# A two-block vision network on one core: half of the first token half's fc1 by fifteen products on quarters

## The chip, the cores and the metric

The kernel runs on one core of one Trainium2 chip. The metric is device microseconds of the whole program. The core has a matrix engine (TensorE, PE in the profile, with its weight loads as PEld), VectorE (DVE), ScalarE (ACT), GpSimd (POOL) and SyncE (SP); SP and POOL also issue transfers.

## The reference

Eight images of 384 channels and 32 x 32 points go through two layers, all in f32. Tokens are the points of an image, 1024 of them.

```
xn  = layernorm(x)                                  # over 384 channels
q, k, v = xn @ w_qkv.T + b_qkv                      # 8 heads of 48
x1  = x + softmax(q k.T / sqrt(48)) v @ w_proj.T + b_proj
h   = gelu(layernorm(x1) @ w_fc1.T + b_fc1)         # 1536 wide
x   = x1 + h @ w_fc2.T + b_fc2

y   = depthwise 7x7 convolution of x + dw_b
y   = gelu(layernorm(y) @ w1 + b1)                  # 1536 wide
y   = gamma * y * (|y| / mean |y|) + beta + y       # |y| over the tokens of a channel
out = x + y @ w2 + b2
```

## The kernel before, in words

Channels lie on the 128 partitions, three tiles of them (`CT`), and tokens along the rows. The 1536 hidden channels are twelve tiles. [...]

**Order of the work.** Python writes the instructions out in the order in which each engine runs them; there is no other scheduler. `Flow` keeps a planned time: every matrix product advances it (`flow.pe(U)`, U = 0.857 us for 512 columns), and side work is written as generators ("chains") that yield the time until their next step. A step is put into the engines' queues where the planned time has come. `flow.finish(chain)` issues all that is left of a chain at once.

**An image's round.** For image b: q and k, attention (64 steps), fc1, fc2; then w1 of image b - 1, the values of b + 1, w2 of b - 1, and so on. The convolution of an image (`convolution`, on VectorE, one tap after another over three channel tiles) is started by `start_conv` after its layer 1 is done and runs beside the next image's round, at a planned pace; `help_convolution` takes the last `HELPED` taps of each channel tile: ScalarE multiplies (`tap`), a POOL transfer adds into `acc`.

**fc1, in `mlp` (line 919).** For each token half the twelve tiles are computed by `gelu_half` (line 891): three products of 512 columns into an o bank (four of them), then ScalarE's gelu to `hid`. After tile 3 of the first half `rest()` ends attention and adds its projection (`proj`), and the layernorm of the second half is spawned (`layernorm`, line 501: sums L482 on TensorE, L525, squares, variance L482, ScalarE's L552 and L553, and three scalings L556 on VectorE). `behind_ln` is `conv_norm` (line 1770): when this layernorm has ended, `norm_of_next` starts the layernorm of the next image (four additions L1838, L1840, folds on POOL), and `end_soon` (line 1803) finishes the convolution before the layernorm of its result.

**Products by thirds.** q, k and w1 are already computed by `tiles_by_thirds` (line 422): three tiles times two token halves, in fifteen products for eighteen. The right-hand sides are sums of token halves (`make_thirds`, ten VectorE operations), the weights are sums of weight blocks (`sums_singly`, in image 0, kept in HBM as `s_qk`, `s_w1`). The products come in this order, and accumulate in four banks:

```
SINGLY = (6, 10, 3, 5, 12, 2, 0, 11, 1, 4, 14, 7, 9, 8, 13)
BANKS = {"n": (6, 5, 0, 4, 9), "z": (12, 11, 14, 8), "k": (10, 7), "q": (2, 1), "j": (3,), "m": (13,)}
```

`SUMS` says what is read from a bank after each product. Copies (`c11=n`) go to ScalarE, sums (`c31=n+c31`) to VectorE (L447, L450); j, q and m share the bank x. A product that writes to a bank waits for the last read of it.

**The shift of w1, in image 0.** `shift_through_w1` (line 1575) folds a bias through w1 in two rounds: load 1152 KB on POOL's queue, pause 22.0, six VectorE operations (L1584, L1586), two folds by POOL transfers (L1588), pause 8.0, then `two_sums` on TensorE (L287). In attention of image 0, just before the first `proj`, `attention` finishes both the `folding` and the `aside` chains, of which this is one.

**Weights.** SP loads weight chunks into a ring of nine buffers, in the order of a plan; a chunk's buffer is given back when its last product is written out (`weights.used`).

Of the kernel before, what the change touches and what calls it, by code (L numbers as in the profile page):

```python
# [67 lines left out]
HELPED = 7  # L68
# [107 lines left out]
def block_kernel(  # L176
# [11 lines left out]
    w1t: bass.AP,  # L188
    w2: bass.AP,
# [15 lines left out]
    quiet = []  # L205
    exact = [False]
# [3 lines left out]
    s_w1 = dram.tile([P, HT // CT, len(FORMS), P], F32, tag="s_w1", bufs=1, name="s_w1")  # L210

# [126 lines left out]
    def plan_fc1(tag):  # L338
        return [((f"fc1_{tag}", c), chunk(wfc1, c)) for c in range(NC)]
# [57 lines left out]
    def thirds_of(src, spare):  # L397

        b11, b12, b21, b22, b31, b32 = (src[:, s, half(n)] for s in range(CT) for n in range(2))
        f, h, e2, g = averages()  # L400
        e, f2, h2, g2, f3, d = (spare[:, s, half(n)] for s in range(CT) for n in range(2))
        steps = (
            (e, b11, b12, ALU.subtract),
            (h, e, b31, ALU.subtract),
            (e2, h, b12, ALU.add),
            (h2, h, b32, ALU.add),
            (f, e, b21, ALU.subtract),
            (g, b22, f, ALU.add),
            (g2, g, b32, ALU.add),
            (f2, f, b12, ALU.add),  # L410
            (f3, f2, g2, ALU.subtract),
            (d, g2, b31, ALU.subtract),
        )
        return steps, (b12, b21, e, b22, f, h, e2, g, b31, f2, h2, g2, f3, b32, d)

    def make_thirds(what, src, us, spare):
        steps, thirds[what] = thirds_of(src, spare)
        for step in steps:
            nc.vector.tensor_tensor(*step)
            yield us  # L420

    def tiles_by_thirds(weights, wname, g, rhs, c, banks, behind):
# [4 lines left out]
        for slot, n in enumerate(SINGLY):  # L427
# [25 lines left out]
            flow.pe(U)  # L453
# [142 lines left out]
    def large_tile(b):  # L596
        if b not in large:
            large[b] = one.tile([P, HT * N], F32, tag="big", name=f"qk_{b}")
        return large[b]

# [161 lines left out]
    def attention(b, xt, qT, kT, last_tile, ready, first, next_image):  # L762
# [44 lines left out]
        for n in range(len(steps) + 2):  # L807
            if n == 2:
                last_tile()
            if n < len(steps):  # L810
                if steps[n][0] == 0 and steps[n][2] == 0:
                    ready(steps[n][1])
                ps[n] = scores(*steps[n])
            if n >= 2:
                product(*steps[n - 2], ps.pop(n - 2))
            if n - 2 in (len(steps) // 2 - 9, len(steps) - 9):
                quiet.append("averages")
            if n - 2 == len(steps) // 2 + 6:
                for chain in first:
                    flow.finish(chain)  # L820
                xn = one.tile([P, CT, N], F32, tag="xn", bufs=2, name=f"xn2_{b}")
                for m in (NP - 1, *range(CT)):
                    flow.finish(chains[0, m])
                proj(b, xt, 0)
                quiet.clear()
                next_image(b)
                slow = {1: 1.35, B - 1: 1.2}.get(b, 1.0)
                fold = "columns" if b else None
                ln = layernorm(xt, xn, 0, eps0, "g2", f"ln2_{b}", False, spaced=True, slow=slow, fold=fold, wait=4.5)
                ln = flow.spawn(ln)  # L830
# [64 lines left out]

    def difference(dst, more, less, direct):
# [22 lines left out]
    def mlp(b, xt, xn, weights, tag, ln, rest, before_fc2=None, behind_ln=None):  # L919

        hid = one.tile([P, HT * N], F32, tag="big", name=f"hid_{b}").rearrange("p (m n) -> p m n", m=HT)
# [3 lines left out]
        for m in range(HT):  # L925
            gelu_half(hid, m, 0, xn, weights, wa, f"fc1_{b}")
            if m == 3 and rest:
                rest()
                slow = 1.2 if b == 1 else 1.0
                ln = flow.spawn(layernorm(xt, xn, 1, eps0, "g2", f"ln2_{b}", True, slow=slow))  # L930
                behind_ln(ln)
        flow.finish(ln)
# [176 lines left out]
    def convolution(acc, us, first=(), y0=0, y1=H, ready=tuple(range(CT)), taken=None, helped=0):  # L1109
# [5 lines left out]
        taps = KS * KS - helped  # L1115

        shares = [size(*divmod(i, KS), y0, y1) for i in TAPS[:taps]]
        shares = [taps * s / sum(shares) for s in shares]
        while min(done) < taps:
            left = [c for c in ready if done[c] < taps and not (taken and taken.get(c, 0) > flow.now)]  # L1120
            if not left:
# [18 lines left out]
    def help_convolution(acc, us, taken):  # L1140

        yield 8.0
        for ct in reversed(range(CT)):
            taken[ct] = float("inf")
            for i in TAPS[KS * KS - HELPED :]:
# [356 lines left out]
    def prepare(weights, aside):  # L1502
# [72 lines left out]
        def shift_through_w1():  # L1575
            for i in range(0, HT // 2, CT):
# [12 lines left out]
                yield 8.0  # L1589
# [124 lines left out]
    def main():  # L1714
# [21 lines left out]
        for b in range(1, B):  # L1736
            if b < B - 1:
                plan += plan_fc1(b) + plan_fc2_fast(b)
# [25 lines left out]
        def start_conv(b, us, *first):  # L1764
# [3 lines left out]
            state["help"] = flow.spawn(help_convolution(acc, 2.7, taken), paced=True)  # L1768
# [21 lines left out]
        def sums_for_tiles(i):  # L1790
            width = len(FORMS) * P
            spare = large[0][:, (2 * NP + 2 * i) * N : (2 * NP + 2 * i + 2) * N]
            for w, store, g in ((wqkt, s_qk, i), (w1t, s_w1, i), (w1t, s_w1, i + 2)):
                yield from sums_singly(w[:, g * width : (g + 1) * width], store[:, g : g + 1], spare)
                yield 8.0

# [121 lines left out]
        for b in range(B):  # L1918
# [9 lines left out]
            if b == 0:  # L1928
                for chain in singly:
                    flow.finish(chain)  # L1930
            if b < B - 1:
# [8 lines left out]
            if b == 0:  # L1940
                xt = load_x(b + 1, "x")
                flow.finish(preparing)
                start_conv(b, 1.6, (9, 1.65), (10, 24.0))
# [5 lines left out]
            if b < B - 1:  # L1949
                flow.finish(state["w1"])  # L1950
                y, gx = grn_up(b - 1, weights, b - 1)
                start_conv(b, 1.6 if b == B - 2 else 1.65, (23, 2.4), (24, 9.0), (25, 26.0))
# [117 lines left out]
def _arrays(i):  # L2070
# [19 lines left out]
    def in_thirds(a, places):  # L2090
# [19 lines left out]
        "w1t": in_thirds(i["L1_conv_w1"], [[4 * r + g for g in range(4)] for r in range(CT)]),  # L2110
        "w2": columns(i["L1_conv_w2"]),
# [19 lines left out]
```

## Time and profile before

| what | value |
|---|---|
| time, median of 3 runs | 3225.36 us (3224.21 to 3226.81) |
| the profiled execution's own time | 3222.53 us |
| its span, first to last instruction | 3220.8 us |
| mean granted TensorE clock | 0.999 |
| TensorE busy | 3205.4 us, 100% |
| VectorE busy | 2470.9 us, 77% |
| ScalarE busy | 1670.8 us, 52% |
| GpSimd busy | 513.1 us, 16% |
| fc1 records on TensorE (L393, `fc<-xn,fc`) | 1152 of 512 columns, 504.3 us |
| VectorE's convolution taps (L1135, `acc`) | 861, mean 1157 ns |

Lines of the profile name the engine, the source line (L393 is line 393 of the kernel), the operation and what is written from what. An f32 matrix product is two records. Records overlap in time, so a product's cost is read from the distance between starts: 0.858 us for 512 columns in a long row of them. VectorE's operations overlap a little too: a 512-column addition is shown with 0.69 us, and the next one starts 0.6 us after it.

### The profile page before, as it was taken

To read this page: it belongs to the slowest core of one execution; us is meant where nothing else is said; L and a number is where in the kernel's file an instruction comes from. 1 tells how busy PE (TensorE), PEld (TensorE's weight loads), DVE (VectorE), ACT (ScalarE), POOL (GpSimd) and SP (SyncE) were. 2 spreads that over 40 slices of the span, in tenths; PEclk is the share of its full clock that TensorE was granted. 3 is DMA by queue.
4 is the path that set the end of the run, shared out by engine and by line. 5 is a ranking of instruction groups with operands and counts; after the bars stand their busy time and mean duration, and the time that the engine had idled before them with its cause. 6 is when DMAs were issued, how large, how long until landed. Compare 5 with 4: busy or idle time off the path is not lost. (4 is left out here: it accounts for less than half of the span.)

```text
span 3220.8 us, 38808 instructions
## 1 busy us (share of the span) xinstructions
PE 3205.4 (100%) x14084; PEld 1375.1 (43%) x14084; DVE 2470.9 (77%) x3375; ACT 1670.8 (52%) x2353; POOL 513.1 (16%) x609
## 2 busy tenths in 40 slices
PE   9999999999999999999999999999999999999999
PEld 5334434443344433444344443444434444344454
DVE  4537788787877878778787687876878778879964
ACT  3542763457644475444753637637365374732543
POOL 2101211112120121201212011220121202200000
PEclk9999999999999999999999999999999999999999
DMA  6524742647335573446636375363843638433234
GB/s 217 168 82 153 167 88 58 161 111 176 80 70 157 125 157 77 95 138 153 138 66 120 113 186 107 66 130 105 200 95 59 149 98 205 73 84 90 59 119 109
DMA packets 205857, 386.64 MB, mean 120 GB/s; under 512 B 42592, under 2 KB 49120, under 8 KB 205280
## 3 DMA queue, kind: packets, MB, share of 16 engines
q0 software_dynamic: 83424, 166.76, 27.7%
q1 hardware_dynamic: 121952, 216.66, 21.9%
q8 instruction: 113, 1.85, 0.2%
q10 hardware_dynamic: 288, 0.71, 0.1%
q14 instruction: 80, 0.66, 0.1%
HBM read 201.18 MB, written 38.14 MB: 74 GB/s over the span
## 5 line engine op out<-in xcount | busy, mean ns | idle before, releaser
L1135 DVE SCALAR_TENSOR_TENSOR acc<-pad,vec,acc 128x870 f32<-128x870 f32 (+8 forms) x861 | 964.1, 1157 | 6.8 <-DMA acc<-tap 1.7
L782 ACT ACTIVATE p<-s 128x1024 f32<-128x1024 f32 x512 | 524.0, 1024 | 254.7 <-PE s L773 247.9
L773 PE MATMUL s<-qk 48*64 48x512 f32 x4096 | 537.2, 591 | 0.2 <-ACT qk L619 0.2
L793 PE MATMUL o<-p,v 64*64 64x512 f32 x4096 | 534.9, 590 | 0.0
L393 PE MATMUL fc<-xn,fc 128*128 128x512 f32 x1152 | 504.3, 594 | 0.0
L1157 POOL DMA_DIRECT2D acc<-tap x294 | 252.5, 873 | 1413.4 <-ACT tap L1156 722.8
L393 PEld LDWEIGHTS fc<-xn,fc 128*128 128x128 f32 x1152 | 217.2, 190 | 278.2 <-issue 267.7
L460 PE MATMUL fc_p<-hid,fc 128*128 128x512 f32 x728 | 316.8, 593 | 0.0
L472 ACT ACTIVATE hid<-fc,bfc_f 128x512 f32<-128x512 f32 x192 | 130.8, 684 | 331.5 <-PE fc L393 331.4
L460 PE MATMUL o_p<-y,w 128*128 128x512 f32 x664 | 289.0, 593 | 0.0
L793 PEld LDWEIGHTS o<-p,v 64*64 64x64 f32 x4096 | 162.1, 133 | 277.6 <-issue 271.7
L773 PEld LDWEIGHTS s<-qk 48*64 48x64 f32 x4096 | 158.8, 133 | 279.0 <-issue 225.4
L1156 ACT ACTIVATE tap<-pad,vec 128x512 f32<-128x512 f32 x294 | 215.8, 734 | 1.5 <-DMA acc<-tap 1.3
L460 PEld LDWEIGHTS fc_p<-hid,fc 128*128 128x128 f32 x728 | 137.8, 190 | 173.3 <-issue 168.3
L460 PEld LDWEIGHTS o_p<-y,w 128*128 128x128 f32 x664 | 125.7, 190 | 157.7 <-issue 143.4
L1135 DVE SCALAR_TENSOR_TENSOR acc_last<-pad,vec,acc_last 128x377 f32<-128x377 f32 (+24 forms) x288 | 177.3, 692 | 0.6
L734 DVE TENSOR_TENSOR attn<-o,attn 128x512 f32<-128x512 f32 x64 | 44.2, 690 | 141.2 <-ACT attn L732 141.2
L906 ACT COPY pad<-x 128x512 f32<-128x512 f32 x42 | 26.4, 634 | 196.2 <-DVE x L983 196.2
L715 PE MATMUL proj<-attn,wproj_sb 128*128 128x512 f32 x288 | 127.1, 595 | 0.0
L693 PE MATMUL v<-wv_sb,xn 128*128 128x384 f32 x384 | 126.8, 487 | 0.0
L447 DVE TENSOR_TENSOR y<-h_n,y 128x512 f32<-128x512 f32 x72 | 49.8, 692 | 64.3 <-PE h_n L431 62.0
L693 PEld LDWEIGHTS v<-wv_sb,xn 128*128 128x128 f32 x384 | 72.5, 190 | 50.1 <-issue 3.3
(397 smaller groups left out, 4089.3 us busy)
## 6 DMA issues: line engine op xcount, KB each, us to landing
acc<-tap POOLq DMA_DIRECT2D x294, 256.0 KB, 3.6
fc<-s_fc SPq DMA_DIRECT2D x91, 256.0 KB, 3.1
w<-s_w SPq DMA_DIRECT2D x91, 256.0 KB, 2.7
w<-s_w SPq DMA_DIRECT2D x72, 320.0 KB, 3.0
fc<-in_wfc SPq DMA_DIRECT2D x54, 384.0 KB, 4.4
y<-y POOLq DMA_DIRECT2D x38, 512.0 KB, 6.6
hid<-hid POOLq DMA_DIRECT2D x36, 512.0 KB, 7.2
qk<-s_qk SPq DMA_DIRECT2D x42, 320.0 KB, 4.9
```

The costliest lines, as they stand in the source:

```text
L393: nc.tensor.matmul(out=ps, lhsT=lhsT(k), rhs=rhs(k)[:, half(h)], start=(k == 0), stop=(k == nk - 1))
L447: nc.vector.tensor_tensor(c[dst], banks(name), c[other], ALU.add)
L460: nc.tensor.matmul(out=bank, lhsT=lhsT, rhs=rhs, start=k == 0, stop=k == len(pairs) - 1)
L472: nc.scalar.activation(dst, src, function, **kw)
L693: nc.tensor.matmul(out=ps[:, :C], lhsT=xn[:, k, t * P : (t + 1) * P], rhs=wv_sb[:, k, :], start=(k == 0), stop=(k == CT - 1),)
L715: nc.tensor.matmul(out=ps, lhsT=wproj_sb[:, m, ct * P : (ct + 1) * P], rhs=attn[:, m, :], start=(m == 0), stop=(m == CT - 1),)
L773: nc.tensor.matmul(out=s[64 * i : 64 * i + 64, j, :], lhsT=kT[64 * j : 64 * j + HD, m, k0 : k0 + 64], rhs=qT[64 * j : 64 * j + HD, m, half ...
L782: nc.scalar.activation(p, s, AF.Exp)
L793: nc.tensor.matmul(out=outs[i][64 * j : 64 * j + 64, :], lhsT=v[keys, t, at : at + 64], rhs=p[keys, j, :], start=(t == 0), stop=(t == KT - 1),
L1135: nc.vector.scalar_tensor_tensor(dst, window, tap, dst, ALU.mult, ALU.add)
L1156: nc.scalar.mul(t.rearrange("p (h w) -> p h w", w=W), window, tap)
L1157: nc.gpsimd.dma_start(out=acc[:, ct, half(h)], in_=t, accum_op=ALU.add)
```

## The change

Images 1 to 6 get a different fc1 for tiles 6 to 11 of the first token half. The half is cut in two quarters of 256 columns. `make_quarters` makes ten sums of quarters on VectorE, right behind the layernorm of the first half (still beside attention), into parts of the hidden tile that aren't used yet. `gelu_group` runs `tiles_by_thirds` on three tiles: fifteen products of 256 columns, with banks of two kinds (n and k in o banks, x and z in the s banks of attention); the sums land in `hid`, and gelu is taken in place. Group 0 (tiles 6 to 8) stands first, right after attention; then come plain tiles 0 to 5, with `rest()` now after tile 1; then group 1 (tiles 9 to 11). The second half stays as it was. While `hold` isn't empty (from `rest()` to tile 4) the convolution's chain issues no taps.

The weight sums for this (`sums_for_fc1`) are made in image 0, 22.0 after attention, in the tile `v`, and kept in HBM as `s_fc1`; after that POOL sets `v` to 1.0 again. Six chunks of them join the plan of each image. `hid` is now the same tile as q and k of the image.

Besides: the first of the two rounds of `shift_through_w1` pauses 18.0 rather than 8.0 between fold and sums. `HELPED` becomes 6, 7, 7 (channel tile 0 gives one tap back to VectorE). The helped taps come every 2.5 rather than 2.7, and the convolution's paces are set anew.

```diff
-HELPED = 7
+HELPED = 6, 7, 7
...
+    def fast_fc1(b):
+        return not exact[0] and 0 < b < B - 1
...
+        sums = plan_singly(f"fc1t_{tag}", s_fc1)
+        return sums[:3] + raw[:3] + sums[3:] + raw[3:]
...
+    def make_quarters(src, hid, us):
+
+        blocks = [src[:, s, quarter(n)] for s in range(CT) for n in range(2)]
+        places = [hid[:, 8 + i // 2, quarter(2 + i % 2)] for i in range(8)]
+        places[2:2] = [hid[:, 10, quarter(0)]]
+        places[6:6] = [hid[:, 10, quarter(1)]]
+        steps, thirds["fc1"] = thirds_of(blocks, places)
+        for step in steps:
+            nc.vector.tensor_tensor(*step)
+            yield us
...
                 ln = layernorm(xt, xn, 0, eps0, "g2", f"ln2_{b}", False, spaced=True, slow=slow, fold=fold, wait=4.5)
+                if fast_fc1(b):
+                    ln = sequence(ln, make_quarters(xn, hidden(b), 1.5))
...
+    def gelu_group(hid, g, b, weights):
...
+        def bank(name):
+            name = "x" if name in "jqm" else name
+            if name not in tiles:
+                make = o_tile if name in "nk" else s_tile
+                tiles[name] = make(f"fc1_{b}_{g}_{name}")[:, : NH // 2]
+            return tiles[name]
+
+        def gelu(r):
+            m = 6 + 3 * g + r
+            other_table(hid[:, m, half(0)], hid[:, m, half(0)], AF.Gelu, bias=bfc1[:, m : m + 1])
+
+        def behind(n):
+            if n == 14:
+                gelu(2)
+
+        c = {f"c{r + 1}{n + 1}": hid[:, 6 + 3 * g + r, quarter(n)] for r in range(CT) for n in range(2)}
+        for _ in tiles_by_thirds(weights, f"fc1t_{b}", g, thirds["fc1"], c, bank, behind, U / 2):
+            pass
+        gelu(1)
+        gelu(0)
...
-        for m in range(HT):
+        for m in range(HT // 2 if fast else HT):
+            if fast and m == 0:
+                gelu_group(hid, 0, b, weights)
             gelu_half(hid, m, 0, xn, weights, wa, f"fc1_{b}")
-            if m == 3 and rest:
+            if m == (1 if fast else 3) and rest:
                 rest()
                 slow = 1.2 if b == 1 else 1.0
+                if fast:
+                    hold.append(b)
                 ln = flow.spawn(layernorm(xt, xn, 1, eps0, "g2", f"ln2_{b}", True, slow=slow))
                 behind_ln(ln)
+            if m == 4:
+                hold.clear()
+        if fast:
+            gelu_group(hid, 1, b, weights)
         flow.finish(ln)
...
-            if not left:
+            if not left or hold:
                 yield 1.0
                 continue
...
-                yield 8.0
+                yield 8.0 if i else 18.0
...
-            state["help"] = flow.spawn(help_convolution(acc, 2.7, taken), paced=True)
+            state["help"] = flow.spawn(help_convolution(acc, 2.5, taken), paced=True)
...
+        def sums_for_fc1():
+            width = len(FORMS) * P
+            spare = v.rearrange("p t w -> p (t w)")
+            for g in range(2):
+                yield from sums_singly(wfc1t[:, g * width : (g + 1) * width], s_fc1[:, g : g + 1], spare)
+                yield 8.0
+            for t in range(KT):
+                nc.gpsimd.memset(v[:, t, :], 1.0)
...
+                fc1_sums = flow.spawn(after(None, sums_for_fc1(), 22.0))
...
-                start_conv(b, 1.6, (9, 1.65), (10, 24.0))
+                flow.finish(fc1_sums)
+                start_conv(b, 1.6, (9, 1.6), (10, 20.0), (48, 1.45))
...
-                start_conv(b, 1.6 if b == B - 2 else 1.65, (23, 2.4), (24, 9.0), (25, 26.0))
+                start_conv(b, 1.65 if b == B - 2 else 1.8, (23, 2.4), (24, 9.0), (25, 20.0), (62, 1.5))
```

In the changed kernel the line numbers are others: the group's products are L456, its sums L472 and L475, plain fc1 tiles L404, gelu L497, taps L1202, the layernorm's scalings L581, the next image's additions L1914 and L1916, the shift's sums L294.

## Prediction

> **What bounds the kernel now.** I read the page's busy shares first, then TensorE's own waits, then time lines of the stretches that the change touches.
>
> ```profile
> PE 3205.4 (100%) x14084; PEld 1375.1 (43%) x14084; DVE 2470.9 (77%) x3375; ACT 1670.8 (52%) x2353; POOL 513.1 (16%) x609
> ```
>
> A busy TensorE may still run below its pace, so its waits decide:
>
> ```profile
> PE b L287 <- DMA w_lnb<-w_lnb: 5.4, 1, 5.4
> PE warm L1728 <- POOL eps L1716: 1.1, 1, 1.1
> ```
>
> All its other waits are 1.0 us or less. It is the bound from end to end: a product taken out is worth its own time, and a wait put in costs its full length.
>
> In images 1 to 6 the place of the change looks like this (image 2; TensorE, then ScalarE, then VectorE; start, length, line, operation):
>
> ```profile
> 899.98 7.03 PE L393 MATMUL fc<-xn,fc 128*128 128x512 f32 x16
> 906.85 1.02 PE L482 MATMUL ln_var<-ln_sq,ones 128*128 128x512 f32 x2
> 907.70 28.49 PE L393 MATMUL fc<-xn,fc 128*128 128x512 f32 x66
> ```
>
> ```profile
> 907.75 1.28 ACT L468 ACT_TABLE_LOAD   x1
> 909.05 0.69 ACT L552 ACTIVATE ln_rstd<-ln_var,eps 128x512 f32<-128x512 f32 x1
> 909.76 0.63 ACT L553 ACTIVATE ln_rstd<-ln_rstd 128x512 f32<-128x512 f32 x1
> ```
>
> ```profile
> 910.43 2.08 DVE L556 SCALAR_TENSOR_TENSOR xn<-xn,vec,ln_rstd 128x512 f32<-128x512 f32 x3 [5.04 <-ACT ln_rstd L553]
> 912.42 1.28 DVE L1838 TENSOR_TENSOR ln<-xn 128x512 f32<-128x512 f32 x2
> 913.63 1.28 DVE L1840 TENSOR_TENSOR ln<-ln,xn 128x512 f32<-128x512 f32 x2
> 914.83 15.27 DVE L1135 SCALAR_TENSOR_TENSOR acc<-pad,vec,acc 128x899 f32<-128x899 f32 x13
> ```
>
> When the layernorm of the second token half ends, VectorE gets a block of 19.7 us in one piece (910.43 to 930.13): the scaling, four additions of the next image's layernorm, and the convolution's remaining 13 taps, which `end_soon` issues at once. TensorE meanwhile runs 66 fc1 records without a break, because plain fc1 tiles need ScalarE's gelu and nothing of VectorE. That is the cover which the change takes away.
>
> [...] after TensorE's one long wait:
>
> ```profile
> 101.54 1.04 PE L773 MATMUL s<-qk 48*64 48x512 f32 x8
> 107.97 1.96 PE L287 MATMUL b<-ones,w_lnb 64*128 64x1 f32 x12 [5.38 <-DMA w_lnb<-w_lnb]
> 109.86 1.99 PE L793 MATMUL o<-p,v 64*64 64x512 f32 x8
> 111.62 1.93 PE L773 MATMUL s<-qk 48*64 48x512 f32 x8
> ```
>
> A group of eight that takes 0.86 us elsewhere takes 1.75 here. [...] the 256-column L525 shows 418.
>
> **The parts.** TensorE's pace: w1's products by the same scheme start every 0.858 us at 512 columns. At 256 columns:
>
> ```profile
> 9.38 2.75 PE L1651 MATMUL ln_sum<-xn,ones 128*128 128x256 f32 x12
> ```
>
> Twelve records are six products; less the last one's tail of 0.17 us that is 0.430 us each. Weight loads take 190 ns, a half product 215, so they stay hidden.
>
> *Products.* Per image 18 x 0.858 = 15.44 us go, 30 x 0.430 = 12.90 come: 2.54 saved, **15.2 us** over six images (11.6 if a product takes 0.45).
>
> *Group 0*, first after attention. In the changed program's VectorE queue its eleven sums stand among the attention's last addition, a wait on `r`, a reciprocal and three taps: addition, tap, x, n, z, r-product, tap, n, reciprocal, n, tap, z and the rest (x, n, z: the bank read). Bank n is accumulated into by products 1, 4, 7, 10, 13, and each must wait until the last sum was read from it. In the trace the addition starts 0.7 us after the last attention product; start to start a 512-column operation takes 0.6, a tap 1.05, a 256-column one 0.34 (0.42 less the same overlap). x is read by 2.7 where product 6 would start at 2.15 (0.6 lost), the second n by 5.5 where product 10 would start at 4.5 (1.0), z by 7.9 where product 14 would start at 7.2 (0.7). So about 2.4 us an image, **+14.4** (6 to 21): the saving is gone here already.
>
> *Group 1, images 2 to 6.* The same queue reads, from the group's first sum: x, tap, n, z, n, tap, **three scalings, four additions, ten taps**, n, z, k, n, n, z, x. The n after the ten taps reads product 10, and product 13 waits for it. Count from the variance product (L482), 0.858 us long. Two copies out of PSUM now stand ahead of ScalarE's table load; the second waits for product 2 (read by 2.25), so the load comes at 2.25 rather than 0.90 and the scale is ready at 4.9 rather than 3.58. VectorE's own queue reaches the scalings at 6.2. Then 4.4 us (910.43 to 914.83), ten taps at 15.3/13 = 1.18 make 11.8, the n sum 0.4: 22.8. Product 13 was due at 0.858 + 12 x 0.430 = 6.0. **16.8 us an image, +84** (71 with taps at 1.05 and the scalings at 4.9; 87 at most). Queued behind product 13 are two products and the whole second half of fc1.
>
> *Group 1, image 1.* Its layernorm is slower (1.2), so the scalings stand after the last n that TensorE waits for. But the last x stands behind 17 taps, `gelu(0)` needs it, and the second half's gelus are queued behind it on ScalarE. VectorE gets to that x about 33 us after product 1. TensorE waits 1.3 us for the scalings, then fills the four o banks by 19.4, and the fifth tile waits for a gelu that comes at 34.7: **+16.6** (12 to 19).
>
> *Clock.* [...] The trace's own: work worth 0.83 + 2.14 us took 6.09 after it, 3.1 lost. **+18.6** (10 to 20).
>
> *The first fold's longer pause.* Now: TensorE waits at 102 for the fold that lands at 107.83 and 108.39; with the half clock it costs 8.7 us (114.06 against 102.43 + 2.97). Ten microseconds later the fold has long landed, so these 8.7 go. But the second round starts ten later too: its pause of 22 then ends 0.6 us after `attention` finishes the chain, so scalings, fold and sums are issued back to back just ahead of proj. In the trace they had room:
>
> ```profile
> 133.90 0.48 DVE L1584 TENSOR_SCALAR w_lnb<-w_lnb,vec 128x384 f32<-128x384 f32 x1
> ...
> 136.12 1.27 DVE L1586 SCALAR_TENSOR_TENSOR w_lnb<-w_lnb,vec 128x384 f32<-128x384 f32 x2
> 137.30 0.20 DVE L741 RECIPROCAL inv<-sums 128x8 f32<-128x8 f32 x1
> 143.93 0.69 DVE L760 TENSOR_TENSOR attn<-attn,r 128x512 f32<-128x512 f32 x1 [6.43 <-DMA r<-back]
> ```
>
> ```profile
> 137.69 1.00 POOL L1588 DMA_DIRECT2D w_lnb<-w_lnb  x1 [0.65 <-DVE inv L741]
> ```
>
> In the changed queue these scalings stand behind the last r-product, which needs reciprocal plus 6.4 us: about 134 with everything 8.7 earlier. Scalings 3.5, POOL's issue 0.3, landing some 3 us: 141. TensorE arrives at 143.86 - 8.7 = 135.2: some 6 us, and 2 to 3 of half clock. **0 net** (-6 to +6): the wait changes place.
>
> *The rest, at 0.* Quarters: ten additions of 0.34 us an image during attention, spaced by 1.5; VectorE idles 1.86 us at its end. Sums for fc1 in image 0: 40 small operations of 0.2 us, two loads and two stores of 960 KB on POOL's queue, eight memsets of 0.44; they start 22 us after attention, under fc1 tiles that don't need VectorE, and fc1 lasts 62 us; the s_w2 stores queued behind are read an image later. Without that cover up to 5. Six more weight loads an image on SP: the ring is nine deep and filled during attention. Tap counts 6, 7, 7 put one tap (1.1) more on VectorE and take two ScalarE taps (0.73) and two POOL DMAs off. Paces and hold move taps among stretches: all together -3 to +5.
>
> **Sum.** -15.2 + 14.4 + 84 + 16.6 + 18.6 + 0 = +118.4 on the profiled execution's 3222.5 (span 3220.8) gives 3340.9; the median of the runs shown is 2.8 higher, at 3225.4. I take 3342. All low ends: +78 or so, 3300; all high ends: 3370.
>
> **Rivals.** (a) *Faster*: the block on VectorE is through before the sums need it, because the convolution has no taps left when the layernorm ends. Then only the 15.2 count, or nothing after group 0: 3207 to 3222. It decides where both groups together wait 2.5 us an image; group 0 alone comes to 2.4, so past it even one tap ahead of the sums is too many, and the queue holds ten. Against it is also that the scalings ahead of them can't start before the variance product. 3%. (b) *Half a stall*: something lets n be read early, 8 us an image: 3222.5 + 118.4 - 5 x 8.8, 3297. Nothing in the queue speaks for it. 6%. (c) *More waits behind the wait*: after it fc2's products meet POOL's folds or ScalarE's backlog, 6 us an image: 3378. Against it: those steps are placed by planned time and gain slack while TensorE stands. 8%. (d) The shift's pause only moves its wait: counted above.
>
> **Numbers.** Forecast 83%; range 3300 to 3370 leaves out (a), (b), (c) and little else. About 0.2% (6.5 us) is what a measurement can tell: faster 3%, within 2%, slower 95%.
>
> **What would show it.** TensorE's waits: product L456 on VectorE's L472, five times some 16 us; in image 1 L404 on ScalarE L497, some 15. Half clock after each. VectorE: ten L1202 in one piece with an idle TensorE. Group 0: waits of 1 us or less. L294 on `w_lnb` now in the second round. A TensorE without waits over 5 us in the fc1 stretches would make this wrong.

## The result and the profile after

The changed kernel takes **3365.95 us** (median of 4 runs, 3365.05 to 3367.83), the kernel before beside it 3224.78 (3223.45 to 3226.81). The ratio is **1.0438, 95% interval 1.042 to 1.0456**: slower by 141 us. The profiled execution took 3365.05 us, its span is 3363.3.

The busy shares and the granted clock (tenths, in 40 slices) of the changed kernel's page:

```profile
PE 3226.7 (96%) x14228; PEld 1399.5 (42%) x14228; DVE 2543.0 (76%) x3610; ACT 1691.1 (50%) x2399; POOL 506.8 (15%) x607
...
PEclk9899999999989999899998999999999999999999
```

TensorE is busy for 21 us more, although 15 us of products went (worked out below), in part because some of it runs at half clock: behind the wait of image 2 shown below the granted clock was 0.50 from 965 to 969 us, 0.72 up to 971, then 1.00. A slice is 84 us; the four eights are the slices of image 0's attention and of fc1 in images 2, 3 and 4. Its waits (line, what ended the wait; us in total, times, longest):

```profile
PE fc_n L456 <- DVE qk L472: 81.2, 17, 14.5
PE fc L404 <- ACT qk L497: 14.6, 1, 14.6
PE s L801 <- ACT qk L647: 10.3, 7, 2.7
PE b L294 <- DVE attn L762: 6.6, 1, 6.6
PE b L294 <- DMA w_lnb<-w_lnb: 4.2, 2, 3.5
PE fc_z L456 <- DVE qk L472: 3.6, 5, 0.7
PE fc_x L456 <- DVE qk L472: 2.5, 6, 1.0
```

The first line holds the forecast wait for product 13, five times 14.5 us, and short waits of both groups; the second is the forecast wait for gelu in image 1. The third (L801, attention's first products, on ScalarE's L647, which adds the bias to q or k) and the fourth (L294, the sums of the shift, on VectorE's L762, an addition of attention) were not forecast. Group 1 of image 2, TensorE and then VectorE (start, length, line, operation; in brackets the idle time before it and what ended it):

```profile
949.93 0.59 PE L456 MATMUL fc_k<-qk,fc1t 128*128 128x256 f32 x2
965.03 1.22 PE L456 MATMUL fc_n<-qk,fc1t 128*128 128x256 f32 x2 [14.50 <-DVE qk L472]
966.04 1.06 PE L456 MATMUL fc_z<-xn,fc1t 128*128 128x256 f32 x2
```

```profile
949.68 2.07 DVE L581 SCALAR_TENSOR_TENSOR xn<-xn,vec,ln_rstd 128x512 f32<-128x512 f32 x3
951.67 1.29 DVE L1914 TENSOR_TENSOR ln<-xn 128x512 f32<-128x512 f32 x2
952.87 1.29 DVE L1916 TENSOR_TENSOR ln<-ln,xn 128x512 f32<-128x512 f32 x2
954.08 10.57 DVE L1202 SCALAR_TENSOR_TENSOR acc<-pad,vec,acc 128x899 f32<-128x899 f32 x10
964.55 0.42 DVE L472 TENSOR_TENSOR qk<-fc_n,qk 128x256 f32<-128x256 f32 x1
```

Product 13 starts 0.06 us after that last line ends. It waited for one sum of 0.42 us, which stood behind three scalings, four additions and ten taps, though the product that this sum reads had started at 949.07.

In image 1 the group's last sum stands behind seventeen taps, and the gelu of its tile behind that sum, and with it all later gelus, which give the o banks back (VectorE, ScalarE, TensorE):

```profile
543.99 17.86 DVE L1202 SCALAR_TENSOR_TENSOR acc<-pad,vec,acc 128x870 f32<-128x870 f32 x17
561.78 0.41 DVE L472 TENSOR_TENSOR qk<-fc_x,qk 128x256 f32<-128x256 f32 x1
```

```profile
562.23 0.72 ACT L497 ACTIVATE qk<-qk,bfc_f 128x512 f32<-128x512 f32 x1 [20.13 <-DVE qk L472]
```

```profile
563.58 2.08 PE L404 MATMUL fc<-xn,fc 128*128 128x512 f32 x2 [14.64 <-ACT qk L497]
```

To see where the 142 us lie, I compared the start of each stage on TensorE in the two traces. The lag of the changed kernel grows by:

| stage | lag gained, us |
|---|---|
| image 0, attention to fc1 | 9.45 |
| fc1 of images 1 to 6 | 17.75, 18.19, 18.79, 18.35, 18.40, 16.82: 108.3 |
| fc2 of images 1 to 6 | 2.22, then 0.5 to 0.9 each: 5.5 |
| q and k of images 2 to 7 | 1.3 to 2.7 each: 10.5 |
| attention of images 1 to 6 | 0.7 to 3.3 each: 9.3 |
| all else | -0.3 |

Of the 2.22 in fc2 of image 1 some 1.1 are work that moved there: eight records of the convolution's layernorm (L521) that stood in fc1 in the kernel before.

### The profile page after: what moved, and what is told of

Same layout as the page of the kernel before. It is cut to its first block, busy times and chain, and to the rows that moved or that the text cites. A ratio compares the mean times of both kernels' runs of the same rounds, so it can differ in the third digit from the quotient of the medians.

```text
span 3363.3 us, 39551 instructions
## 1 busy us (share of the span) xinstructions
PE 3226.7 (96%) x14228; PEld 1399.5 (42%) x14228; DVE 2543.0 (76%) x3610; ACT 1691.1 (50%) x2399; POOL 506.8 (15%) x607
## 4 chain that ended last, share of the span: by engine, by line
PE 77%; DVE 8%; issue 5%; DMA 4%; ACT 2%; POOL 1%; SPq 0%; DVEq 0%; POOLq 0%; ACTq 0%
PE fc L404 13%; PE s L801 11%; PE o L821 11%; PE fc_p L485 10%; PE o_p L485 5%; DVE acc L1202 4%; PE proj L743 4%; DMA acc<-tap 3%; PE v L721 3%; PE h_n L456 3%; PE h_z L456 2%; PE h_x L456 2%; PE o L1310 2%; PE h L391 2%; PE h_last L1359 2%
## 5 line engine op out<-in xcount | busy, mean ns | idle before, releaser
L1202 DVE SCALAR_TENSOR_TENSOR acc<-pad,vec,acc 128x930 f32<-128x930 f32 (+8 forms) x868 | 968.9, 1155 | 6.2 <-DMA acc<-tap 4.6
L801 PE MATMUL s<-qk 48*64 48x512 f32 x4096 | 547.7, 593 | 11.0 <-ACT qk L647 10.3
L404 PE MATMUL fc<-xn,fc 128*128 128x512 f32 x936 | 417.3, 601 | 14.6 <-ACT qk L497 14.6
L1224 POOL DMA_DIRECT2D acc<-tap x280 | 241.4, 875 | 1165.8 <-DVE gscale L1388 501.7
L801 PEld LDWEIGHTS s<-qk 48*64 48x64 f32 x4096 | 158.8, 133 | 297.2 <-issue 215.0
L404 PEld LDWEIGHTS fc<-xn,fc 128*128 128x128 f32 x936 | 179.7, 193 | 238.7 <-issue 218.0
L485 PE MATMUL fc_p<-qk,fc 128*128 128x512 f32 x624 | 273.6, 594 | 0.7 <-DVE qk L1050 0.7
L485 PEld LDWEIGHTS fc_p<-qk,fc 128*128 128x128 f32 x624 | 117.5, 190 | 151.4 <-issue 146.5
L1202 DVE SCALAR_TENSOR_TENSOR acc_last<-pad,vec,acc_last 128x377 f32<-128x377 f32 (+24 forms) x288 | 177.1, 688 | 0.6
L497 ACT ACTIVATE qk<-fc,bfc_f 128x512 f32<-128x512 f32 x108 | 73.8, 687 | 191.6 <-PE fc L404 191.6
L762 DVE TENSOR_TENSOR attn<-o,attn 128x512 f32<-128x512 f32 x64 | 44.1, 689 | 113.3 <-ACT attn L760 112.1
L1928 DVE SCALAR_TENSOR_TENSOR xn<-ln_sum,xn 128x256 f32<-128x256 f32 (+1 forms) x54 | 23.2, 503 | 114.6 <-PE ln_sum L1908 114.6
L456 PE MATMUL fc_n<-qk,fc1t 128*128 128x256 f32 x96 | 33.2, 430 | 77.7 <-DVE qk L472 77.7
```

What stands on the lines that cost most here:

```text
L404: nc.tensor.matmul(out=ps, lhsT=lhsT(k), rhs=rhs(k)[:, half(h)], start=(k == 0), stop=(k == nk - 1))
L456: nc.tensor.matmul(out=at, lhsT=weights.at(wname, g, slot // 5)[:, slot % 5, :], rhs=rhs[n], start=first, stop=True, skip_group_check=not ...
L485: nc.tensor.matmul(out=bank, lhsT=lhsT, rhs=rhs, start=k == 0, stop=k == len(pairs) - 1)
L497: nc.scalar.activation(dst, src, function, **kw)
L801: nc.tensor.matmul(out=s[64 * i : 64 * i + 64, j, :], lhsT=kT[64 * j : 64 * j + HD, m, k0 : k0 + 64], rhs=qT[64 * j : 64 * j + HD, m, half ...
L1202: nc.vector.scalar_tensor_tensor(dst, window, tap, dst, ALU.mult, ALU.add)
```

## The experiments

Every time below stands against runs of the kernel before on the same chip; the ratio and its 95% interval are given. Two experiments whose times are compared can stem from different chips, on which the kernel before took 3224.7 to 3226.1. "Lag" is again that of a stage against the kernel before.

### The block behind group 1

```diff
                 if fast:
                     hold.append(b)
+                    gate.append(b)
...
         if fast:
             gelu_group(hid, 1, b, weights)
+        gate.clear()
...
+        def gated(chain):
+            while gate:
+                yield 1.0
+            yield from chain
...
-                    state["norm1"] = flow.spawn(after(ln, norm_of_next(b, 22.0 if b > 1 else 28.0)))
-                    state["norm3"] = flow.spawn(after(ln, sequence(end_soon(b), norm)))
+                    state["norm1"] = flow.spawn(after(ln, gated(norm_of_next(b, 22.0 if b > 1 else 28.0))))
+                    state["norm3"] = flow.spawn(after(ln, gated(sequence(end_soon(b), norm))))
```

> The changed kernel, but the four additions of the next image's layernorm and the rest of the convolution's taps are issued only after group 1's last gelu, no longer between its sums. Theory (the wait is for the place of these steps in VectorE's queue): of the five waits of 14.9 us in images 2 to 6 only what the three scalings cost stays, some 1 to 3 us each, and image 1's 15.2 us wait for gelu goes; the half clock after them (about 3 us each) goes with them: 75 to 105 us less than the changed kernel's 3366, so 3261 to 3291. Rival (the sums of a group are too slow for fifteen products on quarters, whatever stands between them): group 1 would still wait 8 us or more an image, and the time stay above 3320. Second rival (the steps that are moved back now hold up the two layernorms after fc2): the waits of fc1 go, but TensorE waits as long further on, and the time stays above 3340.

Measured: 3283.5 us, ratio 1.0175 (1.016 to 1.0191), 82 us less than the changed kernel. TensorE's waits in this kernel (its lines stand one lower):

```profile
PE fc_n L457 <- DVE qk L473: 16.8, 17, 1.6
PE s L802 <- ACT qk L648: 8.0, 6, 2.9
PE h_n L457 <- ACT y L478: 7.0, 6, 1.2
PE b L295 <- DVE attn L763: 5.6, 1, 5.6
PE fc_p L486 <- DVE qk L1053: 4.2, 6, 0.8
```

The longest wait of fc1 falls from 14.5 to 1.6, and image 1's wait for gelu is gone. The lag of the six fc1 stages falls from 108.3 to 17.3. So the forecast mechanism holds, and the rival that the group is too slow by itself falls. The second rival is true in small: what was moved back costs 10.1 in fc2 (`fc_p`) and 7.3 in w1 (`h_n`), where the changed kernel lost 5.5 and nearly nothing. The other lags, image 0's 8.1 and 19 in q and k and attention, did not go with the fc1 waits. They have causes of their own.

### Group 0 alone

```diff
-        for m in range(HT // 2 if fast else HT):
+        for m in (*range(6), *range(9, HT)) if fast else range(HT):
...
-        if fast:
-            gelu_group(hid, 1, b, weights)
```

> The changed kernel, but tiles 9 to 11 are three plain tiles again in their old place (18 products of 512 columns); group 0, quarters, hold, paces and the longer pause stay. Theory (group 1 holds the waits): group 1's saving of 1.3 us an image goes, and its waits of 14.9 us and the half clock after them too: fc1 of images 1 to 6 is 0 to 2 us an image longer than in the kernel before. Left are image 0's 9.5 and, if they don't follow from group 1, the 20 us of q and k and attention: 3234 to 3262. Rival (group 0's own waits are larger than the 2.4 us an image of the prediction, or the layernorm that now starts after tile 1 stalls plain tiles too): above 3275.

Measured: 3265.11 us, ratio 1.0119 (1.0103 to 1.0134), 3 us above what the theory gave. The fc1 stages lag by 7.3 in all, 1.2 an image: half the products' saving, less than what group 0's waits cost. The block of ten taps is still there, as long as ever (10.56 us), but plain tiles run beside it and TensorE doesn't stop. Image 0 lags by 7.3 and q and k and attention by 24.6, the part that I had put too low.

### The convolution's numbers of before

```diff
-HELPED = 6, 7, 7
+HELPED = 7, 7, 7
...
-            state["help"] = flow.spawn(help_convolution(acc, 2.5, taken), paced=True)
+            state["help"] = flow.spawn(help_convolution(acc, 2.7, taken), paced=True)
...
-                start_conv(b, 1.6, (9, 1.6), (10, 20.0), (48, 1.45))
+                start_conv(b, 1.6, (9, 1.65), (10, 24.0))
...
-                start_conv(b, 1.65 if b == B - 2 else 1.8, (23, 2.4), (24, 9.0), (25, 20.0), (62, 1.5))
+                start_conv(b, 1.6 if b == B - 2 else 1.65, (23, 2.4), (24, 9.0), (25, 26.0))
```

> The changed kernel with the convolution's numbers of the kernel before: helped taps 7, 7, 7 every 2.7, and the old paces. The traces show the stage of q and k later by 1.3 to 2.7 us in each of images 2 to 7 and attention by 0.7 to 3.3, about 20 us in all, which the prediction had at 0. Theory A (the new paces put convolution taps where q and k's and attention's products wait for VectorE): these go, 10 to 20 us less than the changed kernel, 3346 to 3356, with no wait of L801 on L647; the block of taps in group 1 gets no shorter by more than three taps. Theory B (these small waits follow from the late layernorm and the late end of the convolution in fc1): they stay, and the time is within 6 us of 3366.

Measured: 3377.17 us, ratio 1.0469 (1.0455 to 1.0483): 11 us more than the changed kernel, where both theories had less or the same. The trace shows two things at once. No stage of q and k or of attention gains more than 0.02 us of lag: theory A is right on the waits. But fc1's lag is 138.9, 30.6 more, because of this line of VectorE in image 2:

```profile
958.72 15.26 DVE L1202 SCALAR_TENSOR_TENSOR acc<-pad,vec,acc 128x899 f32<-128x899 f32 x13
```

Thirteen taps are left for the block, not ten, and last 15.26 us, not 10.57: 4.7 more in each of five images. In image 1 it is 22 taps in 26.05 us rather than 17 in 17.86, 8.2 more. That makes 31.7, against the 30.6 seen. Here a microsecond more of block is a microsecond more of time. I had allowed for three taps, not for their longer duration (see "The help's pace").

### The pause

```diff
-                yield 8.0 if i else 18.0
+                yield 8.0
```

> The changed kernel with one edit undone: the first round of the shift through w1 pauses 8.0 again between fold and sums. The prediction put this edit at 0 (the wait changes place). The two traces show image 0 later by 9.45 us between attention's start and fc1's end. Theory (the pause causes this): 9 to 10 us less than the changed kernel, 3356 to 3357, and the wait of the sums for the first fold back at some 5.4 us. Rival (something else in image 0, such as the fc1 weight sums, causes it): within 3 us of the changed kernel's 3366.

Measured: 3362.64 us (3358.12 to 3367.51), ratio 1.0422 (1.0408 to 1.0436). The interval overlaps that of the changed kernel, so the time alone settles nothing, and the expected 9 to 10 us did not come. The profiled execution (3365.13 us, as long as the changed kernel's) shows where it went: image 0's lag falls from 9.45 to 0.65, but image 1's fc1 lags by 2.0 more, and the small waits of q and k and attention by 5.4 more (25.3 for 19.9). Why these grew isn't settled. The pause was therefore tried on the kernel before, which has none of them:

```diff
-                yield 8.0
+                yield 8.0 if i else 18.0
```

> The kernel before with one edit of the change: the first round of the shift through w1 pauses 18.0 rather than 8.0. Prediction's term: 0 (-6 to +6). Theory now (while TensorE waits for the fold, VectorE works off some twenty small operations that stood behind a reciprocal; with the longer pause TensorE arrives first, and the sums' bank is read only after them; the second round's fold is then late too): +8 to +11 us, 3233 to 3237, with a wait of L287 on VectorE's attn of 5 to 7 us near 113 and one on w_lnb of 3 to 4 near 149. Rival (it needs the fc1 weight sums or the other edits to do harm): within 3 us of the kernel before.

Measured: 3233.26 us, ratio 1.0027 (1.0016 to 1.0038), **+8.6 us for this one number** (11.6 in image 0 of the profiled execution, 3236.03 us), as the theory had it, though the first wait is longer than its 5 to 7. TensorE's waits:

```profile
PE b L287 <- DVE attn L734: 8.1, 1, 8.1
PE b L287 <- DMA w_lnb<-w_lnb: 4.0, 1, 4.0
```

The changed kernel's own trace shows the mechanism, TensorE first, then VectorE (some of the operations between are left out):

```profile
112.90 0.38 PE L294 MATMUL b<-ones,w_lnb 64*128 64x1 f32 x2
119.85 1.44 PE L294 MATMUL b<-ones,w_lnb 64*128 64x1 f32 x10 [6.57 <-DVE attn L762]
```

```profile
110.57 0.20 DVE L769 RECIPROCAL inv<-sums 128x8 f32<-128x8 f32 x1 [13.44 <-DMA sums<-attn]
...
111.25 1.87 DVE L1527 TENSOR_TENSOR qk<-qk 128x128 f32<-128x128 f32 x7
113.03 0.95 DVE L1674 TENSOR_TENSOR w_gbeta<-w_gbeta,vec 128x768 f32<-128x768 f32 x1
...
119.11 0.68 DVE L762 TENSOR_TENSOR attn<-o,attn 128x512 f32<-128x512 f32 x1
```

VectorE stands 13.44 us at a reciprocal, for a transfer. When that ends at 110.57, 29 small operations are queued up, 8.4 us of work, and behind them the addition L762, which gives back an o bank. The second of the sums' products waits for it. In the kernel before the same addition comes at the same time:

```profile
118.92 0.69 DVE L734 TENSOR_TENSOR attn<-o,attn 128x512 f32<-128x512 f32 x1 [2.06 <-ACT attn L732]
```

But there the sums stand some 10 us of attention earlier in TensorE's order, at 107.97 behind the wait for the fold, and wait for nothing of VectorE. The theory's reason is wrong in one point: the backlog isn't worked off during that wait, it runs from 107.44 to 116.9, for the most part after it. It costs nothing because TensorE, some 8.7 us late through the wait and the half clock behind it (granted clock 0.50 from 108 to 112 us, 0.53 up to 114.06), comes to the addition's own products so late that VectorE then stands 2.06 us for them. With the long pause TensorE isn't late, makes the sums behind those products, at 112.90, and stands for the addition. One delay had covered another.

### The help's pace

```diff
-            state["help"] = flow.spawn(help_convolution(acc, 2.5, taken), paced=True)
+            state["help"] = flow.spawn(help_convolution(acc, 2.7, taken), paced=True)
```

> The changed kernel with one number undone: the helped taps come every 2.7 again rather than 2.5. HELPED, the new paces, hold, both groups and the pause stay. Theory (in the traces a tap on ScalarE stands 1 to 2 us for its buffer, which a POOL addition must give back, and the copy L647 that attention's first products need is queued behind it): the waits of L801 on L647 go, the stages of q and k and of attention are each within 0.5 us of the kernel before, and the time falls by 15 to 20 us, to 3346 to 3351, with no change in the five waits for product 13. Rival (the convolution's new paces or the eighteenth tap on VectorE move these waits): the time stays within 5 us of 3366.

Measured: 3353.32 us, ratio 1.0395 (1.0381 to 1.0409). The waits of L801 on L647 are gone, and no stage of q and k or attention gains over 0.05 us: this one number caused all 19.9 us. ScalarE in the changed kernel, ahead of attention of image 2:

```profile
782.27 0.75 ACT L1223 ACTIVATE tap<-pad,vec 128x512 f32<-128x512 f32 x1 [1.05 <-DMA acc<-tap]
...
786.15 0.74 ACT L1223 ACTIVATE tap<-pad,vec 128x512 f32<-128x512 f32 x1 [2.18 <-DMA acc<-tap]
786.80 1.14 ACT L647 ACTIVATE qk<-qk,bqk 128x1024 f32<-128x1024 f32 x1
```

A tap writes to one of four buffers, which a POOL transfer empties. In this stretch two transfers take 8.4 and 10.1 us from issue (770.99, 772.10) to landing, where the median of all 280 is 3.7; the taps at 779.45 and 782.27 start when these two have landed. At 2.5 us the buffers thus don't come back in time, ScalarE stands at the tap, and L647, which attention's first products need, stands behind it. With 2.7 two transfers of this stretch take 7.9 and 7.7 us, and no tap of it waits. All taps together, in the page of the kernel before, of the changed one, and with 2.7 (operations | busy us, mean ns | idle us just before, and what ended it):

```profile
L1156 ACT ACTIVATE tap<-pad,vec 128x512 f32<-128x512 f32 x294 | 215.8, 734 | 1.5 <-DMA acc<-tap 1.3
```

```profile
L1223 ACT ACTIVATE tap<-pad,vec 128x512 f32<-128x512 f32 x280 | 207.1, 740 | 26.0 <-DMA acc<-tap 26.0
```

```profile
L1223 ACT ACTIVATE tap<-pad,vec 128x512 f32<-128x512 f32 x280 | 206.0, 736 | 0.8 <-DMA acc<-tap 0.8
```

The time fell by 13 us, not by 15 to 20, and the waits for product 13 did change. The block, still of ten taps, became longer:

```profile
953.62 11.57 DVE L1202 SCALAR_TENSOR_TENSOR acc<-pad,vec,acc 128x841 f32<-128x841 f32 x10
```

`convolution` picks the channel tiles by which are free of the help. At 2.5 the last ten taps go to tiles in turn; at 2.7 nine of the ten add into tile 0, one after another (read from their forms and starts), and each starts 0.12 to 0.13 us later behind its predecessor than it would behind one of another tile. That is 1.0 in each of five images and 2.4 in image 1 (20.29 against 17.86), 7.4 of the 8.3 us by which fc1's lag is larger here.

### Other orders: is there a version that gains?

First the order of the change, with taps held during both groups, the block behind group 1, and the pause, help and paces of before:

```diff
+                hold.append(b)
                 gelu_group(hid, 0, b, weights)
+                hold.clear()
...
-            if m == 4:
-                hold.clear()
         if fast:
             gelu_group(hid, 1, b, weights)
+            hold.clear()
+        gate.clear()
```

> The changed kernel with its order of groups and tiles, but: the additions of the next layernorm and the rest of the taps only after group 1, as in the first experiment; taps held during the two groups (group 0 from its first to its last product, group 1 from rest() to its last sum) and not between; the pause, HELPED, the help's 2.7 and the paces of the kernel before. Theory: image 0's 9 us and q and k's and attention's 20 us go; in fc1 only the scalings' wait is left, 0 to 3 us an image over the saving; fc2 and w1 wait some 2 us an image for what was moved back, as in the first experiment: 3226 to 3250. Rival (the taps now left to one block behind group 1 are many more than eight, and fc2's differences and the third layernorm wait for them): fc2 and w1 later by 6 us an image or more, above 3255.

Measured: 3255.83 us, ratio 1.0098 (1.0082 to 1.0113): the rival's range, but by one image alone. fc1's lag is 0.9 in all; nearly nothing is lost there. Images 2 to 6 lag some 2.3 each in fc2 and w1, as in the first experiment. Image 1's fc2 lags 16.5, since thirty taps are left for its block: the layernorm of the convolution comes late, with one wait of 9.3 us:

```profile
PE ln_sum L522 <- ACT qk L498: 9.3, 1, 9.3
```

Then both groups ahead of the plain tiles:

```diff
             if fast and m == 0:
+                hold.append(b)
                 gelu_group(hid, 0, b, weights)
-            gelu_half(hid, m, 0, xn, weights, wa, f"fc1_{b}")
-            if m == (1 if fast else 3) and rest:
+                gelu_group(hid, 1, b, weights)
+                hold.clear()
+            if not fast:
+                gelu_half(hid, m, 0, xn, weights, wa, f"fc1_{b}")
+            if m == (0 if fast else 3) and rest:
...
+            if fast:
+                gelu_half(hid, m, 0, xn, weights, wa, f"fc1_{b}")
```

> The changed kernel in another order: group 0 and group 1 both right after attention, the convolution's taps held during these two groups only, then rest(), then the plain tiles 0 to 5, under which the layernorm ends with its block of scalings, additions and taps. The pause, HELPED, the help's 2.7 and the paces are those of the kernel before. Theory (products on quarters save their own time wherever VectorE's queue holds nothing long between the sums, and the block is hidden again under tiles that need nothing of VectorE): the saving of 2.54 us an image less waits of 1 to 3 us an image; image 0 and the stages of q and k and attention as before: 3217 to 3233. Rival (VectorE's wait for the transfer of r, up to 6.4 us in its queue, now stands among group 1's sums, or the gelus of two groups back up on ScalarE and the plain tiles wait for banks): 4 to 8 us an image, 3236 to 3260.

Measured: 3238.8 us, ratio 1.0041 (1.0027 to 1.0054): the rival's range, not the theory's. The block of 13 taps (15.3 us) is under plain tiles again and costs fc1 nothing. But the groups of image 3 take 16.8 us, where thirty products at 0.43 need 12.9 and the plain ones that they replace 15.4. The longest wait, TensorE and then VectorE:

```profile
1291.34 0.70 PE L456 MATMUL fc_n<-qk,fc1t 128*128 128x256 f32 x2 [1.39 <-DVE qk L472]
```

```profile
1290.26 0.69 DVE L788 TENSOR_TENSOR attn<-attn,r 128x512 f32<-128x512 f32 x1 [1.49 <-DMA r<-back]
1290.87 0.42 DVE L472 TENSOR_TENSOR qk<-fc_n,qk 128x256 f32<-128x256 f32 x1
```

VectorE's wait for `r` stood ahead of a sum, as the rival said, if for less than its 6.4. It is not the whole loss, though: fc1 lags by 3.2 in all, fc2 by 9.9 (5.5 of it in image 1) and w1 by 1.8. Why fc2 lags in this order isn't settled. The same order with the new paces and `HELPED = 6, 7, 7`, only the help at 2.7:

> Both groups first, as in the run of that name, but with the new paces and HELPED 6, 7, 7 of the change (the help's 2.7 and the pause 8.0 stay old). Theory (the new paces are worth something only where the block of taps is on the path; with the block under plain tiles they are worth nothing but three taps less behind it): 3232 to 3239 against 3238.8 with the old paces, the gain in the fc2 and w1 stages of image 1. Rival (the new paces put taps between attention's end and group 0's sums): 3240 to 3250.

Measured: 3231.87 us, ratio 1.0022 (1.0013 to 1.0031). That is just below the expected range, but the place that I gave isn't the right one. The profiled executions are 3.4 apart: 1.3 of it lie in image 1's fc2 and w1 (6.1 against 7.4), and 3.5 in fc1 (its lag is -0.3 against 3.2), while image 0 is 1.2 slower. The other half of the 7 us between the medians stays open.

Last, group 0 between the plain tiles 0 and 1, and group 1 right behind rest():

```diff
-            if fast and m == 0:
+            if fast and m == 1:
+                hold.append(b)
                 gelu_group(hid, 0, b, weights)
+                hold.clear()
             gelu_half(hid, m, 0, xn, weights, wa, f"fc1_{b}")
             if m == (1 if fast else 3) and rest:
+                if fast:
+                    hold.append(b)
                 rest()
...
                 behind_ln(ln)
-            if m == 4:
-                hold.clear()
-        if fast:
-            gelu_group(hid, 1, b, weights)
+                if fast:
+                    gelu_group(hid, 1, b, weights)
+                    hold.clear()
```

> The changed kernel in another order: plain tile 0, group 0, plain tile 1, rest(), group 1, plain tiles 2 to 5; the taps are held during group 0 and from rest() to group 1's end. Pause 8.0 and the help's 2.7 as in the kernel before; HELPED 6, 7, 7 and the new paces as in the changed one. In the run with both groups first, the groups of image 3 took 16.8 us where thirty products at 0.43 need 12.9: three waits of 0.6 to 1.6 us, the longest behind VectorE's wait for r. Theory (the attention's last addition and the wait for r now fall under plain tiles): the groups wait less than 1.5 us an image, so 1 us or more an image stays of the saving: 3212 to 3224, the first version below the kernel before. Rival (the layernorm's short steps and the projection's additions now stand among group 1's sums and cost what r cost, or the block of 25 taps, now under the second half and fc2, makes fc2's differences wait): 3226 to 3245.

Measured: **3219.15 us (21 runs) against 3224.7 (33 runs), ratio 0.9984, interval 0.9977 to 0.999**: inside the theory's range, and the first version below the kernel before. The waits of its groups:

```profile
PE fc_x L456 <- DVE qk L472: 2.6, 7, 0.6
PE fc_z L456 <- DVE qk L472: 1.4, 1, 1.4
...
PE fc_n L456 <- DVE qk L472: 0.8, 5, 0.2
```

The wait for `r` now falls under a plain tile, and the block, now sixteen taps, under TensorE's plain products, which run on through it (image 3, VectorE and then TensorE):

```profile
1311.21 17.09 DVE L1203 SCALAR_TENSOR_TENSOR acc<-pad,vec,acc 128x899 f32<-128x899 f32 x16
```

```profile
1310.66 19.91 PE L404 MATMUL fc<-xn,fc 128*128 128x512 f32 x46
```

fc1 gains 0.6 in image 1, 1.2 to 1.4 in images 2 to 5 and 2.1 in image 6, 7.6 us in all; image 1 gives 3.5 back in fc2 (some 1.1 of it the sums that moved there). Another 0.9 us of the gain stands at the end of the program, as in every run with the new paces; the kernel before with these paces alone wasn't tried.

## Why the prediction was right, and where its sum was off

The direction and the mechanism were right: group 1's sums stand behind a block on VectorE, and the saving is used up by it many times over. The time is 24 us above the forecast of 3342, and two terms lie outside the spread that was given to them: image 0's pause (-6 to +6) and the rest (-3 to +5), together 35 us that the sum did not have. That the time still fell inside 3300 to 3370 is in part luck, since the wait for product 13 and the half clock had been taken 16 us too large. Term by term, from the distances between starts on TensorE:

| term | predicted | measured |
|---|---|---|
| products | -15.2 | -15.0 (60 records at 0.2158 for 36 at 0.4293, six times) |
| group 0's waits | +14.4 | +17.7 (2.8 to 3.1 an image) |
| wait for product 13, images 2 to 6 | +84 | +73.3 (14.67 each) |
| other waits in group 1, images 2 to 6 | none | +5.5 (1.1 each, most before product 7) |
| image 1's fifth plain tile | +16.6 | +14.8, and 2.2 of smaller waits |
| half clock after the six waits | +18.6 | some +13.4 (1.7 to 2.6 each) |
| image 0's pause | 0 | +9.45 in the traces, +8.6 alone |
| the rest | 0 | +19.9 in q and k and attention, +5.5 in fc2 |

The measured terms add to 147, the spans differ by 142.5: the kernel before had some small waits in these fc1 stages itself, and the 1.1 of moved work stands in fc2's term without being taken out of fc1's. One slip of the prediction's working: with its full saving of 15.2 the low ends add to +75, not +78; the result isn't near them.

**The wait for product 13** was 2.1 an image too large, for two reasons. The ten taps took 1.06 each, not 1.18. The 1.18 came from the block of before, which adds into one channel tile thirteen times over; the changed block takes tiles in turn. The prediction had 1.05 as its low end and took the nearer-looking row. And product 13 was itself due 1.1 later, since product 7 had waited. The half clock was sized by the one long wait of before, 5.38 us, with 3.1 lost in the 6.09 us after it; that it would follow each of the six waits was my estimate, for the profile of before has only that one. The trace of the changed kernel shows it after all six: the granted clock was 0.50 until TensorE was back at 1.00, 3.3 to 5.1 us after each wait. The scalings (949.68, that is 6.4 after the variance product's start, predicted 6.2), the block up to the taps (4.40, predicted 4.4) and the sums of 256 columns (taken at 0.42 us; L525 of before is shown with 418 ns at 256 columns, L472 with 0.42 us) were right.

**Image 0** is the first step that failed. "These 8.7 go" was wrong: the fold had landed, but in their new place the sums needed a bank that stood behind VectorE's backlog, and TensorE waited 6.57 us for it. The prediction looked only at what ended the old wait, not at what its delay covered. Its other half held: the second round's sums do wait for `w_lnb` (3.47 and 0.69 us), with half clock behind (0.50 from 151 to 157 us).

**The rest** is the second. "The rest, at 0" counted how many taps the new numbers move, but not what limits a tap's pace: four buffers and a transfer each. The row of before had an idle time of 1.3 us ended by `acc<-tap`, a sign that 2.7 was near the edge. It went unread. That 0.2 us less between taps cost 19.9 us was thus readable in kind, not in size.

Rival (c), six microseconds an image behind the waits in fc2, did not come (0.5 to 0.9 in images 2 to 6). Rival (a), the faster side, named the right condition: its point, some 2.5 us of waits an image for both groups together, is what the last experiment crosses (1.3 in images 2 to 6).

## What to carry to other kernels

Here a product saved on the busiest engine was only worth its time where no sum that it needs stood behind a long block in another engine's queue; put such a scheme where that queue holds short work, and the block under work that needs nothing of it. Before a wait is taken away, look at what the other engines get done in the time that it costs. Before steps are paced faster, look for idle time that ends on their own buffer.

## What the runs showed of the hardware that I had not expected

In these runs a tap that added into the channel tile of the tap before it started later than one that changed tiles: for the same form (128x870) 1.035 us from start to start in the changed kernel's block, 1.16 in the block with the help at 2.7 and in that of the kernel before, with the operation itself shown with 1.12 in each. So it started some 0.04 after its predecessor's end rather than 0.09 before it.

The half clock did not follow from a wait's length alone here. The wait of 1.82 us ahead of attention of image 3 was followed by some 6 us at half clock; the granted clock by stretches of 2 us (us, PE busy and records, then PEl, DVE, ACT, POOL, the clock, DMA's share, GB/s):

```profile
1200.00:1202.00 2.00, 0.41 (x4) 0.21 (x8) 2.00 (x4) 1.53 (x2) 0.84 (x1) 1.00 1.03 273
1202.00:1204.00 2.00, 2.00 (x16) 0.42 (x8) 2.00 (x4) 1.92 (x2) 0.85 (x1) 0.56 0.96 169
1204.00:1206.00 2.00, 2.00 (x6) 0.83 (x3) 0.83 (x1) 1.99 (x3) 0.84 (x1) 0.50 0.71 124
1206.00:1208.00 2.00, 2.00 (x3) 0.34 (x1) 0.69 (x1) 1.73 (x3) 0.85 (x1) 0.50 0.97 164
```

The same wait in image 7 was 2.67 us long and left the clock at 1.00 (2858 to 2868 us). What tells the two apart wasn't tried.
